# A Mamba block with two gated layers: what follows the scan, from its first norm on, one tick later, and a broadcast copy moved from VectorE to ScalarE

## The chip, the cores and the metric

The kernel runs on one core of a Trainium2 chip. A core has five engines that each work through their own instruction stream in order: TensorE (PE in the profile; its weight loads are PEld), VectorE (DVE), ScalarE (ACT), GpSimd (POOL) and SyncE (SP), which here issues nearly all DMAs. [...] The metric is device time in microseconds (us) of one execution. Before the change three runs gave 1165.02, 1166.05 and 1168.84 us; the median is 1166.05 us.

## What is computed

The input is 4 sequences of 1024 tokens with 256 features, all float32. Cut to what matters:

```python
x = x + mamba_block(layernorm(x))
x = x + ffn(layernorm(x))

# mamba_block(v):
#   u = rmsnorm(v);  z, xs, B, C, dt_raw = split(u @ in_proj)
#   dt = softplus(dt_raw @ dt_proj + b)
#   for each token t:   h = exp(dt_t * A) * h + (dt_t * xs_t) * B_t     (8192 states per sequence)
#                       y_t = sum over states of h * C_t
#   h1 = v + ((y + xs * D) * silu(z)) @ out_proj
#   return h1 + (silu(rms(h1) @ gate) * (rms(h1) @ up)) @ down          (704 hidden)
# ffn(v):  (hadamard(silu(v @ W1) * (v @ W3))) @ W2                     (1024 hidden)
```

The Hadamard transform is folded into W2 at the start (the tile `w2h`), so that it costs nothing later.

## The kernel before

**Units and ticks.** The 4 x 1024 tokens are cut into 8 units of 512 tokens, two per sequence (`us`); units 1, 3, 5 and 7 carry the state on from units 0, 2, 4 and 6. Each unit's scan is cut into 16 steps q of 128 partitions x 4 states x 512 tokens, 128 steps in all. The program is written out by a loop over ticks (L857 to L893), two ticks to a step: tick t belongs to step q = t // 2 and to its first or second half. Unit k is scanned in ticks 32k to 32k+31. This text calls the tick's number within its unit its **place**, 0 to 31.

**What each tick does.** VectorE multiplies the input by B (`times_b`, L765, tile `bx` in PSUM) and runs two scans (`scan`, L774) over two of the step's four states. ScalarE takes the exponentials of the next step, two per tick (`exp`, L741, in place in the tile `da`). GpSimd multiplies the previous step's states by C once per step (`times_c`, L784). TensorE sums them over the states once per step (`sum_states`, L795, eight rows in the trace, tile `py`); that of step q is entered in the second tick of step q+1. SyncE fetches the next tiles: `da` (1 MB, broadcast from memory; four buffers, so the DMA for step q+4 waits for the sum of step q), `ub`, `cr`.

**What else is woven in.** `at(tick, lane, f)` puts a piece of work into a tick, and the lanes say where in the tick it stands: "PE" and "ACT" first, "ACTb" after `times_b`, then the tick's two exponentials; "DVE" stands between the tick's two scans; "POOL" after `times_c`; "PEend" after `sum_states`; "ACTend", "SP" and "SPend" last. Since every engine runs in order, the tick and the lane decide what waits behind what. Two helpers add the dense work:

- `pre(u, H)` prepares the unit that is scanned from tick H on: the norm of x (`un`, L363), its transposes (`transposes`, L213), and projections (`pe_x` and others, through `project`, L226), their copies (`act_x`), and the DMAs that spread them (`dma_xb`, `dma_xr`).
- `post(u, E, other)` finishes a unit whose scan ended at tick E, so it runs beside the next unit's scan: the residual rows (`hr`), the output projection (`wo`, L306 through `add_rows`), the norm's sums (`row_stats`, L173), `small2` on GpSimd, the first normed rows (`hn` with "r3"), their transposes and copies (`ht`), the first gated layer (`gated`, weights `wg`, `wu`, tile `m`), its down projection (`wd`), `small3`, `hn` with "r4", its transposes and copies (`xt`), the second gated layer (`w1`, `w3`, tile `g`), its down projection (`w2h`), and the store.

`gated` takes three chunks at a time: three gate projections, then the `z` projection of a later unit where there is one (`zs`), then three up projections, two to a tick. ScalarE applies SiLU to the three gate projections (`silus`, L263), and copies the up projections out (`up`, L270); GpSimd multiplies (`product`, L274). All projections and transposes go through a ring of four PSUM buffers (`dense`), so a projection waits for the copy of the one four before it.

**The last link of a half unit.** After eight steps `py` is complete. `sum_states` then enters `y_dx` (L810) on VectorE, four ticks after the last step began: at place 18 for the first half of the unit being scanned, at place 2 for the second half of the unit before. `y_z` (L815) follows on GpSimd, and at place 2 and 3 the output projection.

**B's broadcast.** For every half unit the tile `pb` (one PSUM bank, one buffer) gets a copy of the fetched rows `br` (`copy_b`, L754). It may be written only after the last `times_b` of the old half (place 15 or 31), and the first `times_b` of the new one (place 16 or 0) reads it. Before the change VectorE makes the copy at place 15 (between its two scans), ScalarE that at place 31 (lane "ACTb").

Of the kernel before, what the change touches and what calls it, by code (L numbers as in the profile page):

```python
# [11 lines left out]
ALU = mybir.AluOpType  # L12
# [15 lines left out]
def tile_block(ctx: ExitStack, tc: tile.TileContext, a, out):  # L28
# [20 lines left out]
    nc = tc.nc  # L49
# [15 lines left out]
    def dense_psum():  # L65
        return ps_m.tile([P, T], F32, tag="dense", name="dense")
# [14 lines left out]
    us = [{"b": b, "c": c} for b in range(BATCH) for c in range(SEQ // T)]  # L81
# [80 lines left out]
    def row_stats(u, src, ts, centred=True):  # L162

        if 0 in ts:
            u["mv"] = sm.tile([P, 2, TT], F32, tag="mv", name="mv")
        for t in ts:
            junk = p1.tile([P, DM], F32, tag="junk", name="junk")
            nm, ms = u["mv"][:, 0, t : t + 1], u["mv"][:, 1, t : t + 1]
            if centred:
                nc.scalar.activation(  # L170
                    junk, src[:, t, :], AF.Identity, scale=-1.0 / (16 * DM), accum_out=nm
                )
            nc.scalar.activation(  # L173
                junk,
                src[:, t, :],
                AF.Square,
                bias=nm if centred else 0.0,
                scale=1.0 / 16,
                accum_out=ms,
            )  # L180
# [13 lines left out]
    def rsqrt_eps(dst, var):  # L194
        nc.gpsimd.tensor_scalar(dst, var, EPS, 1.0, ALU.add, ALU.mult)
        nc.gpsimd.tensor_tensor(dst, dst, mhalf, ALU.pow)

    def scaled_rows(dst, src, scale, bias, ts):
        for t in ts:
            nc.scalar.activation(  # L200
                dst[:, t, :],
                src[:, t, :],
                AF.Identity,
                bias=bias[:, t : t + 1] if bias is not None else 0.0,
                scale=scale[:, t : t + 1],
            )

    def transposes(u, src):

        u["pt"] = [dense_psum() for _ in range(2)]  # L210
        for k in range(2):
            for t in range(TT):
                nc.tensor.transpose(  # L213
                    u["pt"][k][:, t * P : (t + 1) * P], src[:, t, k * P : (k + 1) * P], ident
                )
# [22 lines left out]
    def at(tick, lane, fn, *args):  # L238
        todo[tick][lane].append(partial(fn, *args))
# [98 lines left out]
    def pre(u, H):  # L338

        s = {}  # L340
# [217 lines left out]
        if H == 32:  # L558

            at(0, "ACTend", lambda: row_stats(u, u["x"], (0, 1)))  # L560
            at(1, "ACTend", lambda: row_stats(u, u["x"], (2, 3)))
            at(3, "POOL", small)
            at(5, "POOL", small_end)
            at(4, "ACT", un, (0, 1))
            at(5, "ACT", un, (2, 3))
            at(6, "PE", lambda: transposes(u, s["un"]))
            at(6, "ACTend", transposed, u, "ut")
        else:
            at(H - 54, "SP", load_x, u)
            at(H - 45, "ACTend", lambda: row_stats(u, u["x"], (0, 1)))  # L570
            at(H - 43, "ACTend", lambda: row_stats(u, u["x"], (2, 3)))
            at(H - 39, "POOL", small)
            at(H - 37, "POOL", small_end)
            at(H - 32, "ACT", un, (0, 1))
            at(H - 31, "ACT", un, (2, 3))
            at(H - 30, "PE", lambda: transposes(u, s["un"]))
            at(H - 30, "ACTend", transposed, u, "ut")
        at(H - 24, "PE", pe_x)
        at(H - 23, "ACT", act_x)
        at(H - 22, "SP", dma_xb)  # L580
        at(H - 19, "SPend", dma_xr, 0)
        at(H - 17, "SPend", dma_xr, 1)
        at(H - 16, "PE", pe_dt)
        at(H - 16, "PE", pe_c, 0)
        if H == 32:
            for h in range(2):
                at(H - 11, "PE", pe_z, h)
# [16 lines left out]
    def post(u, E, other):  # L604


        s = {}

        def hr(ts):
            if 0 in ts:  # L610
                u["hr"] = p2.tile([P, TT, DM], F32, tag="hr", name="hr")
            scaled_rows(u["hr"], u["x"], u["r1"], u["nm1"], ts)

        def small2():
            t = sm.tile([P, 2, TT], F32, tag="s2", name="s2")
            r3 = t[:, 1, :]
            rsqrt_eps(r3, u["mv"][:, 1, :])
            s["r3"] = r3

        def small3():  # L620
            t = sm.tile([P, 2, TT], F32, tag="s2", name="s2")
            nm, r4 = t[:, 0, :], t[:, 1, :]
            nm16, var = u["mv"][:, 0, :], u["mv"][:, 1, :]
            rsqrt_eps(r4, var)
            nc.gpsimd.tensor_tensor(nm, nm16, r4, ALU.mult)
            nc.gpsimd.tensor_scalar(nm, nm, 16.0, None, ALU.mult)
            s["r4"], s["nm"] = r4, nm

        def hn(scale, bias):
            s["tok"] = p1.tile([P, TT, DM], F32, tag="tok", name="hn")  # L630
            scaled_rows(s["tok"], u["hr"], s[scale], s[bias] if bias else None, range(TT))

        def big(name):
            u[name] = p1.tile([P, 8, T], F32, tag="big", name=name)

        def store():
            b, c = u["b"], u["c"]
            nc.sync.dma_start(
                out=out[b, c * T : (c + 1) * T, :].rearrange("(t p) d -> p t d", p=P), in_=u["hr"]
            )  # L640

        at(E + 3, "ACT", hr, (0, 1))
        at(E + 4, "ACT", hr, (2, 3))
        add_rows(
            E + 3,
            u,
            lambda: [u["yt"][:, k, :] for k in range(2)],
            lambda: [W["wo"][:, k, :] for k in range(2)],
            4,
            "PEend",  # L650
            on_pool=u is not us[-1],
        )
        at(E + 5, "ACTend", lambda: row_stats(u, u["hr"], (0, 1), False))
        at(E + 6, "ACTend", lambda: row_stats(u, u["hr"], (2, 3), False))
        at(E + 7, "POOL", small2)
        at(E + 8, "ACT", hn, "r3", None)
        at(E + 9, "PE", lambda: transposes(u, s["tok"]))
        at(E + 9, "ACTend", transposed, u, "ht")
        at(E + 9, "POOL", lambda: nc.gpsimd.tensor_tensor(u["hr"], u["hr"], u["x"], ALU.add))
        at(E + 10, "PE", big, "m")  # L660
        sizes = [min(P, DFF - c * P) for c in range(6)]
        chunks = list(enumerate(sizes))
        for i in range(2):
            gated(E + 10 + 3 * i, u, "m", "wg", "wu", chunks[3 * i : 3 * i + 3], "ht",
                  (other, i) if other else None)
        add_rows(
            E + 18,
            u,
            lambda: [u["m"][:n, c, :] for c, n in enumerate(sizes)],
            lambda: [W["wd"][:n, c, :] for c, n in enumerate(sizes)],  # L670
            1,
        )
        at(E + 20, "ACTend", lambda: row_stats(u, u["hr"], (0, 1)))
        at(E + 22, "ACTend", lambda: row_stats(u, u["hr"], (2, 3)))
        at(E + 23, "POOL", small3)
        at(E + 24, "ACT", hn, "r4", "nm")
        at(E + 25, "PE", lambda: transposes(u, s["tok"]))
        at(E + 25, "ACTend", transposed, u, "xt")
        at(E + 26, "PE", big, "g")
        chunks8 = [(c, P) for c in range(8)]  # L680
        for i in range(3):
            gated(E + 26 + 3 * i, u, "g", "w1", "w3", chunks8[3 * i : 3 * i + 3], "xt")
        add_rows(
            E + 36,
            u,
            lambda: [u["g"][:, c, :] for c in range(8)],
            lambda: [w2h[:, c, :] for c in range(8)],
            1,
            on_pool=u is not us[-1],
        )  # L690
        at(E + 43, "SPend", store)


    an = nega.rearrange("p (h j b a) -> p h j b a", h=2, j=4, b=4)
    NQ = 16 * len(us)
# [52 lines left out]
    def carry_of(s):  # L748
        return s["u"]["carry"][:, s["h"], s["j"], :, s["g"]]

    def copy_b(q):
        u, h = qs[q]["u"], qs[q]["h"]
        u["pb"] = ps_b.tile([P, T], F32, tag="b", name="pb")
        (nc.vector.tensor_copy if h else nc.scalar.copy)(u["pb"], u["br", h])  # L754

    def times_b(q, b0):
        s = qs[q]
# [60 lines left out]
    for k, u in enumerate(us):  # L818
        pre(u, 32 * k)
    for k, u in enumerate(us):  # L820
        post(u, 32 * k + 32, us[k + 2] if k + 2 < len(us) else None)
# [26 lines left out]
        at(10 + i, "PE", hadamard_end, 2 * i)  # L848
    for q in range(8, NQ, 8):
        at(2 * q - 8, "SPend", dma_br, q)  # L850

        at(2 * q - 1, "DVE" if q // 8 % 2 else "ACTb", copy_b, q)

    def has(q):
        return 0 <= q < NQ
# [2 lines left out]
    while todo:  # L858
        q, half = divmod(tick, 2)
# [102 lines left out]
```

## Time and profile before

| | |
|---|---|
| median of three runs | 1166.05 us (1165.02 to 1168.84) |
| the profiled execution | 1173.07 us, span 1171.2 us |
| mean granted TensorE clock | 0.899 |
| first scan of unit 1 to unit 7 begins at | 158.67, 285.07, 415.20, 543.38, 671.46, 800.02, 925.55 us |
| last scan ends | 1053.7 us; the rest is unit 7's `post` alone |
| `times_b` | 1.23 us each, two per step |
| `scan` | 1.21 us (units 0, 2, 4, 6) or 1.27 us (units 1, 3, 5, 7), four per step |
| `times_c` | 4.53 us per step |
| `exp` | 0.71 us, four per step |
| `copy_b` | 0.67 us on VectorE (8), 0.60 us on ScalarE (7) |
| `sum_states` | about 1.0 us per step on a TensorE at full clock |
| one matmul of 128x512 | 0.45 us a row, two rows for each matmul of the code (float32) |
| ScalarE's load of a function table | 1.28 us, 90 in all |

A step lasts 7.4 us in units 0, 2, 4, 6 and 7.65 us in the others where nothing is waited for. In the profile's tables every row has the engine, the line, the operation, out<-in by the program's names, and shapes. In a timeline the first column is the start, the second the duration of a merged group, and the bracket at the end gives how long the engine sat idle before it and what ended that.

### The profile page before, as it was taken

To read this page: it belongs to the slowest core of one execution; us is meant where nothing else is said; L and a number is where in the kernel's file an instruction comes from. 1 tells how busy PE (TensorE), PEld (TensorE's weight loads), DVE (VectorE), ACT (ScalarE), POOL (GpSimd) and SP (SyncE) were. 2 spreads that over 40 slices of the span, in tenths; PEclk is the share of its full clock that TensorE was granted. 3 is DMA by queue.
4 is the path that set the end of the run, shared out by engine and by line. 5 is a ranking of instruction groups with operands and counts; after the bars stand their busy time and mean duration, and the time that the engine had idled before them with its cause. 6 is when DMAs were issued, how large, how long until landed. Compare 5 with 4: busy or idle time off the path is not lost.

```text
span 1171.2 us, 11883 instructions
## 1 busy us (share of the span) xinstructions
PE 959.6 (82%) x3374; PEld 456.5 (39%) x3374; DVE 962.9 (82%) x840; ACT 782.2 (67%) x1411; POOL 887.1 (76%) x515
## 2 busy tenths in 40 slices
PE   8464236969998799969996999979997987799978
PEld 3121012423634255423633364424543362336535
DVE  4897799999998989999999899999999899990000
ACT  3835556868768786779677786878685967563331
POOL 6675758878978888878977998789977898674312
PEclk9777558979899799979998899979997999789989
DMA  7989999898799889997799889988799789730000
GB/s 252 352 300 351 353 327 308 311 325 296 250 340 320 300 298 320 319 327 281 270 348 325 281 300 334 319 325 297 270 310 360 281 291 343 262 111 1 18 0 18
DMA packets 89441, 321.89 MB, mean 275 GB/s; under 512 B 9312, under 2 KB 20000, under 8 KB 73120
## 3 DMA queue, kind: packets, MB, share of 16 engines
q1 hardware_dynamic: 87520, 318.38, 77.1%
q10 hardware_dynamic: 1856, 2.75, 0.7%
q8 instruction: 27, 0.44, 0.1%
q14 instruction: 38, 0.31, 0.1%
HBM read 302.22 MB, written 18.87 MB: 274 GB/s over the span
## 4 chain that ended last, share of the span: by engine, by line
PE 25%; DMA 7%; DVE 6%; POOL 6%; issue 5%; ACT 4%; DVEq 0%; POOLq 0%; ACTq 0%; SPq 0%
PE dense L226 14%; PE dense L306 8%; DMA da<-dtd 5%; POOL da L784 4%; DVE da L774 3%; DVE bx L765 3%; PE py L795 3%; DMA ub<-ud 2%; ACT da L741 1%; POOL m L274 1%; POOL g L274 1%; DVE hr L316 0%; ACT up L270 0%; ACT L741 0%; ACT junk L173 0%
## 5 line engine op out<-in xcount | busy, mean ns | idle before, releaser
L784 POOL TENSOR_TENSOR da<-da,cr 128x2048 f32<-128x2048 f32 x128 | 580.0, 4531 | 86.8 <-DVE da L774 22.5
L741 ACT ACTIVATE da<-da,nega 128x512 f32<-128x512 f32 x508 | 334.4, 713 | 170.8 <-DMA da<-dtd 159.3
L774 DVE TENSOR_TENSOR_SCAN da<-da,carry,bx 128x512 f32<-128x512 f32 x256 | 315.7, 1268 | 20.0 <-DVE bx L765 7.6
L774 DVE TENSOR_TENSOR_SCAN da<-da,bx 128x512 f32<-128x512 f32 x256 | 300.2, 1209 | 37.0 <-ACT da L741 21.3
L765 DVE TENSOR_TENSOR bx<-ub,pb 128x1024 f32<-128x1024 f32 x254 | 312.2, 1229 | 20.3 <-ACT pb L754 9.3
L795 PE MATMUL py<-da,rsel 128*32 128x512 f32 x1024 | 162.5, 712 | 159.4 <-POOL da L784 159.4
L226 PE MATMUL dense<-xt,w 128*128 128x512 f32 x512 | 238.4, 621 | 1.4 <-ACT si L263 1.4
L226 PEld LDWEIGHTS dense<-xt,w 128*128 128x128 f32 x512 | 99.4, 199 | 145.9 <-issue 123.4
L795 PEld LDWEIGHTS py<-da,rsel 128*32 128x32 f32 x1024 | 21.4, 115 | 243.0 <-POOL da L784 201.2
L306 PE MATMUL dense<-w2h,g 128*128 128x256 f32 x512 | 113.4, 380 | 0.0
L274 POOL TENSOR_TENSOR g<-si,up 128x512 f32<-128x512 f32 x64 | 80.5, 1272 | 32.3 <-ACT up L270 32.2
L306 PEld LDWEIGHTS dense<-w2h,g 128*128 128x128 f32 x512 | 96.8, 190 | 18.4 <-ACT ev L321 2.5
L306 PE MATMUL dense<-wd,m 128*128 128x256 f32 (+1 forms) x384 | 98.2, 400 | 0.9 <-POOL m L274 0.9
L316 DVE TENSOR_TENSOR hr<-hr,dense 128x512 f32<-128x512 f32 x20 | 13.4, 669 | 99.9 <-PE dense L306 99.9
L226 PE MATMUL dense<-ut,win 128*128 128x512 f32 x192 | 94.7, 625 | 0.2 <-ACT ut L220 0.2
L270 ACT COPY up<-dense 128x512 f32<-128x512 f32 x112 | 63.4, 579 | 46.8 <-PE dense L226 46.4
L274 POOL TENSOR_TENSOR m<-si,up 128x512 f32<-128x512 f32 (+1 forms) x48 | 60.2, 1270 | 43.5 <-ACT up L270 43.5
L226 PE MATMUL dense<-ht,wg 128*128 128x512 f32 x192 | 87.7, 600 | 3.4 <-ACT ht L220 3.4
L306 PEld LDWEIGHTS dense<-wd,m 128*128 128x128 f32 (+1 forms) x384 | 68.6, 192 | 37.6 <-issue 20.6
L263 ACT ACTIVATE si<-dense 128x512 f32<-128x512 f32 x112 | 60.7, 596 | 28.4 <-PE dense L226 25.5
L226 PE MATMUL dense<-ht,wu 128*128 128x512 f32 x160 | 72.8, 600 | 4.8 <-ACT si L263 4.8
L741 ACT ACT_TABLE_LOAD x44 | 56.5, 1283 | 4.8 <-DMA da<-dtd 4.0
(95 smaller groups left out, 798.6 us busy)
## 6 DMA issues: line engine op xcount, KB each, us to landing
da<-dtd SPq DMA_DIRECT2D x127, 1024.0 KB
ub<-ud SPq DMA_DIRECT2D x254, 512.0 KB
cr<-cd SPq DMA_DIRECT2D x64, 256.0 KB
x<-in_x SPq DMA_DIRECT2D x8, 512.0 KB
dtd<-dt SPq DMA_DIRECT2D x16, 256.0 KB
ud<-du SPq DMA_DIRECT2D x16, 256.0 KB
cd<-cc SPq DMA_DIRECT2D x16, 256.0 KB
out<-hr SPq DMA_DIRECT2D x8, 512.0 KB
```

The costliest lines, as they stand in the source:

```text
L226: nc.tensor.matmul(dst[:n], lhsT=w[:, k, col : col + n], rhs=src[:, k, :], start=(k == 0), stop=(k == 1),)
L263: nc.scalar.activation(g[i]["si"][:n], g[i]["pg"][:n], AF.Silu)
L270: nc.scalar.copy(g[i]["up"][:n], g[i]["pu"][:n])
L274: nc.gpsimd.tensor_tensor(u[dst][:n, c, :], g[i]["si"][:n], g[i]["up"][:n], ALU.mult)
L306: nc.tensor.matmul(po[t // 2][:, t % 2, :], lhsT=left[k][:, t * P : (t + 1) * P], rhs=right[k], start=(k == 0), stop=(k == n - 1),)
L316: nc.vector.tensor_tensor(hr, hr, po[i], ALU.add)
L741: nc.scalar.activation(da, da if q else s["u"]["pdt", b], AF.Exp, scale=an[:, s["h"], s["j"], b, s["g"] : s["g"] + 1],)
L765: nc.vector.tensor_tensor(s["bx"], s["ub", b0 // 2], u["pb"].unsqueeze(1).broadcast_to([P, 2, T]), ALU.mult)
L774: nc.vector.tensor_tensor_scan(da, da, s["bx"][:, b % 2, :], start, ALU.mult, ALU.add)
L784: nc.gpsimd.tensor_tensor(s["da"], s["da"], s["cr"].unsqueeze(1).broadcast_to([P, 4, T]), ALU.mult)
L795: nc.tensor.matmul(u["py"][32 * b : 32 * b + 32, :], lhsT=rsel[:, 2 * s["j"] + s["g"], :], rhs=s["da"][:, b, :], start=first, stop=last,)
```

## The change

For the six units 0 to 5, everything of `post` from the first `hn` on is entered one tick later (`F = E + 1`); what comes before it (`hr`, the output projection, `row_stats`, `small2`) stays, and units 6 and 7 keep all their ticks. The second `hn` goes to lane "ACTend" in those six. In `pre`, for units 2 to 7, `un` and its transposes are entered two ticks later; for units 1 to 7 `pe_x`, `act_x`, `dma_xb`, `dma_xr`, `pe_dt` and the first `pe_c` one tick later. `copy_b` at place 15 is made by ScalarE (lane "ACTb") for units 1 to 6; VectorE keeps it for units 0 and 7. `y_dx`, `y_z` and all of the scan itself keep their ticks.

```diff
@@ pre
-            at(H - 32, "ACT", un, (0, 1))
-            at(H - 31, "ACT", un, (2, 3))
-            at(H - 30, "PE", lambda: transposes(u, s["un"]))
-            at(H - 30, "ACTend", transposed, u, "ut")
-        at(H - 24, "PE", pe_x)
-        at(H - 23, "ACT", act_x)
-        at(H - 22, "SP", dma_xb)
-        at(H - 19, "SPend", dma_xr, 0)
-        at(H - 17, "SPend", dma_xr, 1)
-        at(H - 16, "PE", pe_dt)
-        at(H - 16, "PE", pe_c, 0)
+            at(H - 30, "ACT", un, (0, 1))
+            at(H - 29, "ACT", un, (2, 3))
+            at(H - 28, "PE", lambda: transposes(u, s["un"]))
+            at(H - 28, "ACTend", transposed, u, "ut")
+        at(H - 23, "PE", pe_x)
+        at(H - 22, "ACT", act_x)
+        at(H - 21, "SP", dma_xb)
+        at(H - 18, "SPend", dma_xr, 0)
+        at(H - 16, "SPend", dma_xr, 1)
+        at(H - 15, "PE", pe_dt)
+        at(H - 15, "PE", pe_c, 0)
@@ post: all from here on with F in place of E
-        at(E + 8, "ACT", hn, "r3", None)
+        F = E + (us.index(u) < len(us) - 2)
+        at(F + 8, "ACT", hn, "r3", None)
...
-        at(E + 24, "ACT", hn, "r4", "nm")
+        at(F + 24, "ACTend" if F > E else "ACT", hn, "r4", "nm")
...
-        at(E + 43, "SPend", store)
+        at(F + 43, "SPend", store)
@@
+    def by_vector(q):
+        return q in (8, NQ - 8)
...
-        (nc.vector.tensor_copy if h else nc.scalar.copy)(u["pb"], u["br", h])
+        (nc.vector.tensor_copy if by_vector(q) else nc.scalar.copy)(u["pb"], u["br", h])
...
-        at(2 * q - 1, "DVE" if q // 8 % 2 else "ACTb", copy_b, q)
+        at(2 * q - 1, "DVE" if by_vector(q) else "ACTb", copy_b, q)
```

More of the change, by code (lines that the diff above doesn't have):

```diff
@@ L655, in post @@
         at(E + 7, "POOL", small2)
-        at(E + 8, "ACT", hn, "r3", None)
[L657 to L660, printed above, removed]
+        F = E + (us.index(u) < len(us) - 2)
+        at(F + 8, "ACT", hn, "r3", None)
+        at(F + 9, "PE", lambda: transposes(u, s["tok"]))
+        at(F + 9, "ACTend", transposed, u, "ht")
+        at(F + 9, "POOL", lambda: nc.gpsimd.tensor_tensor(u["hr"], u["hr"], u["x"], ALU.add))
+        at(F + 10, "PE", big, "m")
         sizes = [min(P, DFF - c * P) for c in range(6)]
@@ L663, in post @@
         for i in range(2):
-            gated(E + 10 + 3 * i, u, "m", "wg", "wu", chunks[3 * i : 3 * i + 3], "ht",
+            gated(F + 10 + 3 * i, u, "m", "wg", "wu", chunks[3 * i : 3 * i + 3], "ht",
                   (other, i) if other else None)
         add_rows(
-            E + 18,
+            F + 18,
             u,
@@ L672, in post @@
         )
-        at(E + 20, "ACTend", lambda: row_stats(u, u["hr"], (0, 1)))
-        at(E + 22, "ACTend", lambda: row_stats(u, u["hr"], (2, 3)))
-        at(E + 23, "POOL", small3)
-        at(E + 24, "ACT", hn, "r4", "nm")
-        at(E + 25, "PE", lambda: transposes(u, s["tok"]))
-        at(E + 25, "ACTend", transposed, u, "xt")
-        at(E + 26, "PE", big, "g")
+        at(F + 20, "ACTend", lambda: row_stats(u, u["hr"], (0, 1)))
+        at(F + 22, "ACTend", lambda: row_stats(u, u["hr"], (2, 3)))
+        at(F + 23, "POOL", small3)
+        at(F + 24, "ACTend" if F > E else "ACT", hn, "r4", "nm")
+        at(F + 25, "PE", lambda: transposes(u, s["tok"]))
+        at(F + 25, "ACTend", transposed, u, "xt")
+        at(F + 26, "PE", big, "g")
         chunks8 = [(c, P) for c in range(8)]
         for i in range(3):
-            gated(E + 26 + 3 * i, u, "g", "w1", "w3", chunks8[3 * i : 3 * i + 3], "xt")
+            gated(F + 26 + 3 * i, u, "g", "w1", "w3", chunks8[3 * i : 3 * i + 3], "xt")
         add_rows(
-            E + 36,
+            F + 36,
             u,
```

## The prediction

> **What bounds the kernel now.** I read the page first, then VectorE's waits, then the timelines around the longest of them. The page's first lines:
>
> ```profile
> span 1171.2 us, 11883 instructions
> PE 959.6 (82%) x3374; PEld 456.5 (39%) x3374; DVE 962.9 (82%) x840; ACT 782.2 (67%) x1411; POOL 887.1 (76%) x515
> ```
>
> VectorE and TensorE are equally busy over the span. By stretch it looks different: from unit 1's first scan to the last scan (158.7 to 1053.7 us) VectorE runs almost without a hole, so there every hole is time. The holes, from the view of waits kept to VectorE (total us, times, longest):
>
> ```profile
> DVE da L774 <- ACT da L741: 21.5, 18, 4.2
> DVE yt L810 <- PE py L795: 12.5, 7, 8.9
> ...
> DVE bx L765 <- ACT pb L754: 9.3, 3, 4.1
> ```
>
> The third line is the change's target: at place 0 of units 3, 5 and 7 VectorE waits 3.16, 4.09 and 2.04 us for ScalarE's copy. Of the first line, unit 0 has 15.2 us, and 5.1 us lie at places 14 to 17 of units 2, 4 and 6 (0.70 and 3.05; 0.91; 0.39). The second line looks small (8.9 of it is the tail), but decides. VectorE's timeline where unit 5 begins:
>
> ```profile
> 671.46 1.23 DVE L765 TENSOR_TENSOR bx<-ub,pb 128x1024 f32<-128x1024 f32 x1 [4.09 <-ACT pb L754]
> ...
> 682.90 0.75 DVE L810 SCALAR_TENSOR_TENSOR yt<-xr,dpar,py 128x512 f32<-128x512 f32 x1 [0.95 <-PE py L795]
> ```
>
> After it lost 4.09 us, VectorE still had to wait at `y_dx` for TensorE. In the trace the last row of a half's sum ends 0.15 us before `y_dx` starts six times: at places 18 of units 2, 4, 6 and at places 2 of units 3, 5, 7. So at these six points TensorE's chain sets the time, and a hole filled ahead of them only becomes a longer wait there. At the other `y_dx` the sum is early by 3.68, 3.42, 2.97 us (place 18 of units 1, 3, 5) and 1.12, 0.75, 1.09 us (place 2 of units 2, 4, 6). TensorE's timeline shows why: ahead of `y_dx` it runs in one piece.
>
> ```profile
> 648.99 8.59 PE L226 MATMUL dense<-xt,w 128*128 128x512 f32 x16
> 657.50 1.07 PE L795 MATMUL py<-da,rsel 128*32 128x512 f32 x8
> 658.50 7.13 PE L226 MATMUL dense<-xt,w 128*128 128x512 f32 x16
> 665.57 1.07 PE L795 MATMUL py<-da,rsel 128*32 128x512 f32 x8
> 666.56 7.13 PE L226 MATMUL dense<-xt,w 128*128 128x512 f32 x16
> 673.62 1.07 PE L795 MATMUL py<-da,rsel 128*32 128x512 f32 x8
> 674.62 7.13 PE L226 MATMUL dense<-xt,w 128*128 128x512 f32 x16
> 681.68 1.07 PE L795 MATMUL py<-da,rsel 128*32 128x512 f32 x8
> ```
>
> A step takes 7.4 to 7.65 us, one such group 8.1 us: TensorE falls behind through the second gated layer, and `y_dx` waits for the last sum.
>
> **The change, part by part.** I work in differences to before, at the `y_dx` points.
>
> *Copies.* Six copies leave VectorE: 6 x 0.67 = 4.0 us of work. They stand at place 15, so `y_dx` at place 18 comes next. In unit 1 the sum is 3.68 us early: **-0.7**. Elsewhere they are counted in the next paragraphs. ScalarE gets 6 x 0.60 us. The copy moves behind the last `times_b` of the half, so ScalarE's two exponentials of the tick queue behind it; they are needed two ticks on, which covers it. At place 31 the copy now has neither `silus` nor `up` ahead of it in its tick; the 9.3 us go if the exponentials ahead arrive.
>
> *What stands in front.* The parity matters. The first pair of exponentials of a step waits for its `da` (160 us in the waits of ScalarE); the second pair doesn't. Before, `hn`, `ht`, `xt` and the first `silus` stood ahead of a step's first pair; one tick later they stand behind a first pair. ScalarE's rows around place 26 of unit 3 to 4 and of unit 4 to 5 have the same form:
>
> ```profile
> 646.67 1.04 ACT L220 COPY xt<-dense 128x512 f32<-128x512 f32 x2
> 652.06 2.56 ACT L741 ACTIVATE da<-da,nega 128x512 f32<-128x512 f32 x4 [4.34 <-DMA da<-dtd]
> ```
>
> The copies of `xt` ran, then ScalarE idled 4.34 us for `da`. In the new order they come after that wait. Likewise `small3`'s tick moves past one `times_c` (4.53 us) on GpSimd.
>
> *Place 23 to place 2, into units 2, 4, 6.* Into unit 4: place 23's scans end at 512.05. `times_c` to 516.7, `small3` (1.95) to 518.7, `hn` (2.07) to 520.8, the transposes follow it to about 521.5, but ahead of the copy stand the exponentials that began at 523.02 for want of `da`: one pair to 524.3, the first `xt` copy to 524.9. Four matmuls stand before the next sum (eight before): 8 x 0.45 = 3.6, plus 1.8 from a slow start (8.90 us for the same group at 518.64 against 7.13 warm), to 530.3; then 1.0 and three times 8.07, so the last sum ends at 555.5 where it ended at 552.72. It is 2.8 late against slacks of 1.12, 0.75 and 1.09: 1.7 + 2.0 + 1.7 = **+5.4**. Bounds: 0 if `da` comes 2.8 earlier; +3.3 each if 1.6 later.
>
> *Place 23 to place 2, into units 3, 5, 7.* Before, this took 44.52, 45.45 and 43.40 us, because `times_c` stood behind `small3`, which waited for `row_stats`: at unit 4, GpSimd idled 5.24 us and `times_c` began at 642.54 instead of about 637.5. That goes. The same chain as above from 637.44 gives 47.2 us if `da` lands as before (652.06): 653.4 the pair, 654.0 the copy, 659.4 the matmuls, 684.6 `y_dx`. It gives 41.1 if `da` no longer matters. The middle, 44.2, is about the 44.5 that it was on average: **0**, bounds -3.4 and +2.7 each.
>
> *Place 3 to place 18, units 3 and 5.* The last four up matmuls (3.6) now stand behind the half's last sum, ahead of `wo`, and `un`'s transposes (1.09) between `wo` and `w2h`. In unit 3 the sum ended at 426.49, so: up to 430.1, one sum 431.1, `wo` 3.5, `un` 1.1, `w2h` from 435.7 instead of 433.39: +2.3. `w2h`'s last chunk now waits for one `times_c` more, but only its seventh and eighth matmul need it, and that is just in time (438.3). Then `ht`: equal. Then the first up projection finds all four PSUM buffers taken until a SiLU. That stood ready before; now it follows exponentials whose `da` comes 7.8 to 9.8 us after a sum (457.38 and 473.53 in unit 3): 456.4 + 8.8 + 1.33 + 1.28 + 0.5 = 468.3, while TensorE is there at 466.3: +2.0 (0 to 3.4). Together +4.3, against a slack of 3.42 and 2.97 less the 0.67 of the copy: stalls of 1.55 and 2.0, and with the copy's 0.67 taken off +0.9 and +1.3, **+2.2** (bounds -1.3 and +5).
>
> *Place 3 to place 18, units 2, 4, 6.* No slack here. The same moves cost only +0.2, since `wo` and `w2h`'s first half took 12.0 us there, 1.7 over their 24 matmuls at 0.43. The SiLU wait is again 0 to 3.4, I take 1.8: +2.0 in units 4 and 6. Unit 2 already had such a wait (1.78 us at 350.57): 0. **+4.0** (bounds -1.6 and +8.5). The 5.1 us of waits for exponentials go or are swallowed by this.
>
> *DMAs.* `xbd`, `xr` and the store keep their sizes and pass at most one `ub` on SP's queue. `xr` is read five ticks (18 us) after its issue, more than any wait for `da` above; nothing is late. The tail of units 6 and 7 keeps its ticks: 0.
>
> **Sum.** -0.7 + 5.4 + 0 + 2.2 + 4.0 = +10.9 us. Against the profiled execution: 1173.07 + 10.9 = 1184.0; that one lies 7.0 above the median, so at the median 1166.05 + 10.9 = **1177.0 us**.
>
> [...]
>
> **Rivals.**
> 1. *Faster.* TensorE's chain is not lengthened, because `da` lands before the moved ScalarE work needs it. It decides at `xt`: if `da` is there by the end of the transposes (2.8 us earlier), hardly a term above is positive. For it: four buffers, and the stalls themselves give DMA time. Against it: `da`'s DMA waits for TensorE's own sums. All low bounds: -0.7 + 0 - 10.2 - 1.3 - 1.6 = -13.8, so 1152. Chance 0.33.
> 2. *The holes trade places.* Waits at `pb` turn into equal waits at `y_dx`: 1166. Chance 0.12. A measurement can tell about 0.3% (3.5 us) from no change.
> 3. *The ring.* Later sums make `da` late, and scans wait for exponentials as well; the high bounds, -0.7 + 9.9 + 8.1 + 5 + 8.5 = +30.8, can't all hold, since a wait at one `y_dx` gives time to the chain of the next; two thirds of it, +20.5, gives 1187. Chance 0.12.
> 4. *The change does nothing.* VectorE's stream of the changed kernel holds two copies of `pb` instead of eight, so it does move; ScalarE's holds 90 table loads as before, so nothing is added there. Chance 0.
>
> **How the numbers follow.** My forecast has 0.43, rival 3 0.12: slower 0.55; same 0.12; faster 0.33. To leave out no more than 0.2, the range reaches from rival 1's time to rival 3's: 1152 to 1187. The forecast's own range is 1170 to 1184.
>
> **What would show it.** Right: no wait for `pb` over 1 us; longer waits of `yt` L810 for `py`, at place 18 of units 3 to 6 and place 2 of units 2, 4, 6; TensorE idle before `ht,wu` for `si`; `xt` behind exponentials. Wrong: `yt` waits no longer than before, the 4.0 us of copies show in the steps' length, and units 2, 4, 6 shrink below 126 us.

## The result, and the profile after

The changed kernel takes 1182.99 us (median of four runs, 1178.42 to 1184.42) against 1165.53 us for the kernel before (four runs): a ratio of 1.0138, 95% interval 1.0101 to 1.0175, so it is slower by some 17 us. The profiled execution after took 1183.34 us with a span of 1181.6 us, at a granted clock of 0.897, where before it was 0.899. The page's line of busy times:

```profile
PE 959.4 (81%) x3374; PEld 455.4 (39%) x3374; DVE 959.9 (81%) x834; ACT 786.6 (67%) x1417; POOL 887.3 (75%) x515
```

The work is the same on every engine to 5 us; VectorE has six instructions fewer, ScalarE six more. All of the difference is waiting. VectorE's waits:

```profile
DVE yt L816 <- PE py L801: 34.0, 13, 9.9
DVE da L780 <- ACT da L743: 17.5, 21, 4.8
...
DVE bx L771 <- ACT pb L760: 3.2, 3, 1.5
```

The wait for the copy of B fell from 9.3 to 3.2 us, as it was meant to. The wait of `y_dx` for TensorE's sum rose from 12.5 to 34.0 us; without the tail (8.9 and 9.9) that is 3.6 to 24.1. Six of these waits, 2.84 to 2.95 us each, stand at place 18 of units 1 to 6; the rest, 0.27 to 2.10 us, at place 2 of units 2 to 7. Unit 4's place 18 in VectorE's timeline:

```profile
622.29 0.75 DVE L816 SCALAR_TENSOR_TENSOR yt<-xr,dpar,py 128x512 f32<-128x512 f32 x1 [2.95 <-PE py L801]
```

TensorE's timeline of the same moment, first before, then after: what stands between the half's last two sums, and as the last line the sum that releases `y_dx`:

```profile
610.51 1.98 PE L406 MATMUL dense<-raw,dtw 128*128 128x512 f32 x4
612.34 1.88 PE L226 MATMUL dense<-ut,win 128*128 128x512 f32 x4
614.69 1.06 PE L795 MATMUL py<-da,rsel 128*32 128x512 f32 x8 [0.48 <-POOL da L784]
```

```profile
613.33 3.70 PE L226 MATMUL dense<-ht,wu 128*128 128x512 f32 x8
616.87 1.88 PE L406 MATMUL dense<-raw,dtw 128*128 128x512 f32 x4
619.16 1.98 PE L226 MATMUL dense<-ut,win 128*128 128x512 f32 x4 [0.41 <-ACT up L270]
621.08 1.06 PE L801 MATMUL py<-da,rsel 128*32 128x512 f32 x8
```

Before, 8 rows stood there, and the last sum even waited 0.48 us for GpSimd. After, up projections (`ht,wu`, 8 rows) stand there too, since they moved a tick past the earlier sum, and TensorE is the last to arrive. This is the obvious reading; the first theory below is made of it.

**A ledger.** I cut each unit's cycle in two at TensorE. The **run** goes from the first transpose for `xt` (`hn` with "r4") to the end of the last sum before place 18's `y_dx`; the **way** goes from there to the next `xt` transpose. In it VectorE walks its ticks up to place 23, and `times_c`, `small3` and `hn` follow. Worked out from the traces, means over the five cycles that begin with the `xt` of units 1 to 5's scans; the idle time is the sum of TensorE's pauses of more than 0.15 us:

| profiled execution | its time | run | TensorE idle in it | way | both |
|---|---|---|---|---|---|
| before | 1173.07 | 102.6 | 4.7 | 25.7 | 128.3 |
| after | 1183.34 | 100.3 | 4.4 | 29.5 | 129.9 |

"Both" is by definition the length of a unit, so the ledger explains nothing by itself; it shows where a unit grew. The way is 3.8 us longer, one tick; the run gave 2.3 us back.

Why the way is longer can be read at the end of it. Before, where unit 4's scan runs (all engines, lines of TensorE, GpSimd and ScalarE chosen):

```profile
640.31 0.19 POOL L195 TENSOR_SCALAR s<-mv 128x4 f32<-128x4 f32 x1 [5.24 <-ACT junk L173]
...
642.24 1.09 ACT L200 ACTIVATE hn<-hr,s 128x256 f32<-128x256 f32 x2 [0.31 <-POOL s L626]
...
642.90 0.47 PE L213 MATMUL dense<-ident,hn 128*128 128x128 f32 x1 [5.84 <-ACT hn L200]
```

After:

```profile
644.00 0.19 POOL L789 COPY carry<-da 128x4 f32<-128x4 f32 x1 [3.16 <-DVE da L780]
644.27 4.52 POOL L790 TENSOR_TENSOR da<-da,cr 128x2048 f32<-128x2048 f32 x1
...
648.87 0.19 POOL L195 TENSOR_SCALAR s<-mv 128x4 f32<-128x4 f32 x1
...
650.80 1.09 ACT L200 ACTIVATE hn<-hr,s 128x256 f32<-128x256 f32 x2 [3.14 <-POOL s L626]
...
651.46 0.48 PE L213 MATMUL dense<-ident,hn 128*128 128x128 f32 x1 [0.68 <-ACT hn L200]
```

Before, `small3` (L195) stands ahead of a `times_c` and waits for `row_stats` (5.24 us); the transposes begin at 642.90, which is 27.1 us after the sum (the longest of the five ways before, which go from 23.7 to 27.1). After, `small3` stands behind a `times_c` that starts when VectorE has finished place 23 (643.93; the small copy of `carry` ahead of it waited 3.16 us for that), and ScalarE waits 3.14 us for `small3`; the transposes begin 29.3 us after the sum (622.14). So `xt` now hangs on VectorE's ticks, and VectorE hangs on TensorE's last sum at place 18.

### The profile page after: what moved, and what is told of

Its sections match the earlier page's. It is cut to its first block, busy times and chain, and to the rows that moved or that the text cites. A ratio compares the mean times of both kernels' runs of the same rounds, so it can differ in the third digit from the quotient of the medians.

```text
span 1181.6 us, 11882 instructions
## 1 busy us (share of the span) xinstructions
PE 959.4 (81%) x3374; PEld 455.4 (39%) x3374; DVE 959.9 (81%) x834; ACT 786.6 (67%) x1417; POOL 887.3 (75%) x515
## 4 chain that ended last, share of the span: by engine, by line
PE 42%; ACT 15%; DMA 15%; POOL 9%; DVE 9%; issue 8%; SPq 1%; DVEq 0%; POOLq 0%; ACTq 0%
PE dense L226 27%; PE dense L306 10%; DMA da<-dtd 8%; POOL da L790 7%; ACT da L743 6%; PE py L801 5%; DVE da L780 5%; DVE bx L771 4%; DMA cr<-cd 3%; ACT up L270 1%; ACT L743 1%; ACT L263 1%; DMA ub<-ud 1%; DMA w<-in_w 1%; ACT si L263 1%
## 5 line engine op out<-in xcount | busy, mean ns | idle before, releaser
L801 PE MATMUL py<-da,rsel 128*32 128x512 f32 x1024 | 155.8, 684 | 168.8 <-POOL da L790 168.7
L226 PE MATMUL dense<-xt,w 128*128 128x512 f32 x512 | 245.0, 633 | 3.0 <-ACT xt L220 3.0
L306 PE MATMUL dense<-w2h,g 128*128 128x256 f32 x512 | 115.8, 383 | 6.8 <-ACT ut L220 6.2
L316 DVE TENSOR_TENSOR hr<-hr,dense 128x512 f32<-128x512 f32 x20 | 13.4, 670 | 100.3 <-PE dense L306 100.3
L226 PE MATMUL dense<-ht,wu 128*128 128x512 f32 x160 | 76.4, 617 | 11.1 <-ACT si L263 11.1
L226 PEld LDWEIGHTS dense<-ut,win 128*128 128x128 f32 x192 | 37.7, 205 | 59.6 <-issue 42.6
```

Of the source, the lines that this page charges most:

```text
L226: nc.tensor.matmul(dst[:n], lhsT=w[:, k, col : col + n], rhs=src[:, k, :], start=(k == 0), stop=(k == 1),)
L306: nc.tensor.matmul(po[t // 2][:, t % 2, :], lhsT=left[k][:, t * P : (t + 1) * P], rhs=right[k], start=(k == 0), stop=(k == n - 1),)
L316: nc.vector.tensor_tensor(hr, hr, po[i], ALU.add)
L801: nc.tensor.matmul(u["py"][32 * b : 32 * b + 32, :], lhsT=rsel[:, 2 * s["j"] + s["g"], :], rhs=s["da"][:, b, :], start=first, stop=last,)
```

## The theories

- **P**, the obvious one: the matmuls between the last two sums hold `y_dx` at place 18; take them away, or `y_dx` later, and the time comes back.
- **C**: ScalarE's copies hold its exponentials and `pb`. **L**: late `da` sets the rhythm.
- **D**, a loop: the length of way plus run, of which the second gated layer's tick lengthened the way. It was formed after the first four runs, of which two had spoken against P, with two rivals: **U**, the moves in `pre`, and **A**, the alignment, that is, which work of ScalarE stands behind a pair of exponentials that waits for `da`.

Every kernel is compared with the kernel before on the same chip, whose medians there were 1166.36 us (first four experiments), 1164.24 us (next four) and 1164.91 us (last four).

## The experiments

**The change without its copies.**

```diff
-        return q in (8, NQ - 8)
+        return q // 8 % 2 == 1
```

> The change without its copies: all of the shift by a tick, but VectorE copies pb at place 15 as before. Theory P (TensorE's row ahead of the last sum of place 18 is longer by the shift, and y_dx waits 2.8 to 2.95 us there in units 1 to 6): the copy's 0.67 us falls into that wait, so the time stays within 2 us of the changed kernel, 1181 to 1185 us, with y_dx idle some 2.2 us instead of 2.9 at place 18. Rival C (ScalarE's copy delays the exponentials and pb): the time falls back to about 1166 us.

Measured: 1181.66 us, ratio 1.0126 (1.0106 to 1.0146). The time is as P has it; C falls. The waits of `yt` are 30.7 us instead of 34.0, but not as P has it: at place 18 of units 1, 3 and 5 they are 1.41, 2.86 and 1.90 us, and at that of units 2, 4 and 6 still 2.95. In the changed kernel the copies are worth nothing that can be measured.

**The copies alone.** In the kernel before:

```diff
-        (nc.vector.tensor_copy if h else nc.scalar.copy)(u["pb"], u["br", h])
+        (nc.vector.tensor_copy if q in (8, NQ - 8) else nc.scalar.copy)(u["pb"], u["br", h])
...
-        at(2 * q - 1, "DVE" if q // 8 % 2 else "ACTb", copy_b, q)
+        at(2 * q - 1, "DVE" if q in (8, NQ - 8) else "ACTb", copy_b, q)
```

> The kernel before with only the copies moved to ScalarE in units 1 to 6. Theory P: where the sum was early (place 18 of units 1, 3, 5) 0.67 us is saved each, elsewhere it turns into a longer wait of y_dx: -2 us in all, 1162 to 1166 us. Rival C: the time rises by a good part of the change's 17 us, to 1175 or more. Full worth of the copies: -4.0 us.

Measured: 1171.70 us, ratio 1.0042 (1.0019 to 1.0066). Neither: they cost some 5 us where 2 to 4 were to be gained. Except for the tail and 0.28 us, no `y_dx` waits, and the idle time stands elsewhere:

```profile
DVE bx L765 <- ACT pb L754: 19.6, 6, 4.9
```

All six waits (1.25 to 4.86 us) are at place 16: ScalarE reaches its copy of place 15 late, behind a SiLU, a `zs` and an `up` of the first gated layer, and the last two wait for TensorE (0.45 and 1.18 us in unit 4). The copy was taken off an engine that was waiting and put on one whose queue was longer.

**Projections behind the last sum.** In the changed kernel:

```diff
-        at(H - 15, "PE", pe_dt)
-        at(H - 15, "PE", pe_c, 0)
+        at(H - 14, "PE", pe_dt)
+        at(H - 14, "PE", pe_c, 0)
...
-        at(H - 15, "ACT", act_dt, 0)
-        at(H - 15, "ACT", act_dt, 1)
-        at(H - 14, "ACT", act_c, 0)
-        at(H - 13, "POOL", make_u, 0, nc.gpsimd)
-        at(H - 13, "SPend", dma_dt, 0)
+        at(H - 14, "ACT", act_dt, 0)
+        at(H - 14, "ACT", act_dt, 1)
+        at(H - 13, "ACT", act_c, 0)
+        at(H - 12, "POOL", make_u, 0, nc.gpsimd)
+        at(H - 12, "SPend", dma_dt, 0)
```

> The changed kernel with pe_dt, the first pe_c and what follows them (act_dt, act_c, make_u, dma_dt) one tick later again, so that these four matmuls (3.9 us with their wait) stand behind the last sum of place 18 and no longer ahead of it. Theory P: the six waits of y_dx at place 18 (17.4 us) go, as the sum is 3.9 us earlier and the wait was 2.9; what is left at place 2 is 6.6 us as before: 1183 - 17 = 1166 us, down to 1162 if the copies count as well, up to 1172 if the wait moves to place 2. Rival L (late da sets the rhythm, y_dx only shows it): no more than 4 us of gain, since the scans then wait for da at places 18 and 19.

Measured: 1188.46 us, ratio 1.0184 (1.0156 to 1.0213). The six waits of `y_dx` at place 18 went to 0.00 us, as P says, and the time did not come back: the ratio lies above the change's 1.0138, though the two intervals overlap. (The scan just ahead of `y_dx` waits 1.2 to 1.4 us in units 1, 2, 4, 5 and 6; in the changed kernel it waits 1.42 us in units 2, 4 and 6.) The waits came back at place 2, where `y_dx` now waits 3.51 to 4.24 us in each of units 2 to 7. The trace points to the start of TensorE's run, where TensorE waits for `xt` 20.9 us in five units and waited 2.7 us in the changed kernel (TensorE, then ScalarE):

```profile
658.54 6.12 PE L226 MATMUL dense<-xt,w 128*128 128x512 f32 x7 [4.91 <-ACT xt L220]
```

```profile
656.69 1.33 ACT L743 ACTIVATE da<-da,nega 128x512 f32<-128x512 f32 x2 [4.44 <-DMA da<-dtd]
657.93 1.05 ACT L220 COPY xt<-dense 128x512 f32<-128x512 f32 x2
```

The copies of `xt` stand behind a pair of exponentials whose `da` has not landed (2.29 to 4.92 us in units 1 to 6), the mechanism that the prediction described. P, as the cause of the loss, falls; L's number holds, and here its `da` is seen, though at `xt` and not at the scans of places 18 and 19.

**`y_dx` of place 18 a tick later.** In the changed kernel:

```diff
-            at(2 * q + 4, "DVE", y_dx, u, s["h"])
-            at(2 * q + 5, "POOL0", y_z, u, s["h"])
+            at(2 * q + 4 + (s["h"] == 0), "DVE", y_dx, u, s["h"])
+            at(2 * q + 5 + (s["h"] == 0), "POOL0", y_z, u, s["h"])
```

> The changed kernel with y_dx and y_z of the first half (place 18) entered one tick later; nothing else is moved. Theory P: the tick gives TensorE 3.7 us, more than the wait of 2.9, so the waits at place 18 go and the time is 1166 to 1170 us; the next sum (place 19) needs py freed and starts up to 1.2 us later, which costs nothing on VectorE. Rival L: TensorE and VectorE both hang on late da, the idle time reappears at scans behind it, 1178 us or more.

Measured: 1180.64 us, ratio 1.0124 (1.0101 to 1.0147). Again the waits of `y_dx` at place 18 are gone (0.00 us, the sum over 3.3 us early), and the time has not come back. VectorE waits 34.2 us for exponentials instead of 17.5: in units 2 to 6 at places 18 (0.85 to 1.42 us) and 19 (2.53 to 2.65). Unit 4, VectorE and then ScalarE:

```profile
619.86 1.22 DVE L780 TENSOR_TENSOR_SCAN da<-da,bx 128x512 f32<-128x512 f32 x1 [2.65 <-ACT da L743]
```

```profile
610.91 0.59 ACT L270 COPY up<-dense 128x512 f32<-128x512 f32 x1 [2.37 <-PE dense L226]
...
616.53 1.27 ACT L415 ACTIVATE dt<-dense,dtb 128x512 f32<-128x512 f32 x2
617.81 1.28 ACT L743 ACT_TABLE_LOAD   x1
619.11 1.33 ACT L743 ACTIVATE da<-da,nega 128x512 f32<-128x512 f32 x2
```

L's number (1178 or more) fits, its mechanism doesn't: no `da` is late here. ScalarE's rows stand one behind the other: its `up` waits 2.37 us for TensorE, `act_dt` follows with two table loads (3.83 us), and the exponentials that VectorE needs queue behind. In the changed kernel the same wait lies hidden under that of `y_dx`, 2.95 us. So TensorE's lateness has a second path to VectorE, and takes it once `y_dx` is out of the way.

**The second part back, with a faster `wd`.** In the changed kernel `wd`'s row blocks are entered two to a tick, so that all from the second `row_stats` on can stand in the ticks of before (G = E):

```diff
-            1,
+            2 if us.index(u) < len(us) - 2 else 1,
...
-        at(F + 20, "ACTend", lambda: row_stats(u, u["hr"], (0, 1)))
+        G = E
+        at(G + 20, "ACTend", lambda: row_stats(u, u["hr"], (0, 1)))
...
-        at(F + 24, "ACTend" if F > E else "ACT", hn, "r4", "nm")
+        at(G + 24, "ACT", hn, "r4", "nm")
```

> The changed kernel, but with wd's four row blocks in two ticks instead of four, so that everything from the second row_stats on (small3, hn, xt, the second gated layer, w2h) can stand in the ticks of the kernel before; the first gated layer and pre stay a tick late and the copies stay on ScalarE. Theory D (a loop through xt): from the first xt transpose on TensorE has one almost unbroken run to the last sum at place 18 (100.5 us a unit after the change), and from that sum VectorE's ticks up to place 23, times_c, small3 and hn lead to the next xt (29.5 us, before the change 25.9); a unit lasts as long as the two together. So 29.5 falls back by about 3.6 us in each of five to six units: 1183 - 18 to 22 = 1161 to 1166 us. Theory P (the matmuls ahead of the last sum of place 18): these are unchanged, so at least 1178 us.

Measured: 1190.51 us, ratio 1.0226 (1.0201 to 1.0251). D's size for the way was even exceeded (22.3 us), but the run grew to 110.0 us, with 9.8 us of TensorE's idle time in it. P's number (1178 or more) holds, and the waits at place 18 are still there (2.89 to 2.95 us in units 2 to 6), but P has nothing for a time above that of the changed kernel. D as I had put it, with a run of fixed length, falls. What fills the run (TensorE, then ScalarE):

```profile
593.21 5.73 PE L226 MATMUL dense<-ht,wg 128*128 128x512 f32 x8 [4.63 <-ACT ht L220]
```

```profile
591.36 1.33 ACT L744 ACTIVATE da<-da,nega 128x512 f32<-128x512 f32 x2 [4.17 <-DMA da<-dtd]
```

TensorE is early, but `ht` is still a tick late, behind exponentials that wait for `da`. The first gated layer's tick has its own tie to VectorE's ticks, and it takes over when `xt`'s is loosened.

**The second part alone, a tick late.** In the kernel before, G = E + 1 for units 0 to 5 from the second `row_stats` on, `hn` in lane "ACTend":

```diff
-        at(E + 20, "ACTend", lambda: row_stats(u, u["hr"], (0, 1)))
+        G = E + (us.index(u) < len(us) - 2)
+        at(G + 20, "ACTend", lambda: row_stats(u, u["hr"], (0, 1)))
...
-        at(E + 24, "ACT", hn, "r4", "nm")
+        at(G + 24, "ACTend" if G > E else "ACT", hn, "r4", "nm")
```

> The kernel before with only the part from the second row_stats on (small3, hn, xt, second gated layer, w2h, store) a tick later in units 0 to 5; no copies, first gated layer and pre as before. Theory D: the way from the last sum of place 18 to the next xt grows by up to a tick (3.7 us) in each unit, against which TensorE's run loses the 2 to 4 us in which it waited for times_c: 1170 to 1182 us. Theory P: the matmuls ahead of the sum at place 18 are those of the kernel before, so 1166 us or less.

Measured: 1182.28 us, ratio 1.0143 (1.0118 to 1.0169). This part alone gives a loss as large as that of the change, without copies, without the first layer's up projections between the last sums, and with `y_dx` waiting no more than 0.25 us at place 18. The way is 30.1 us. The waits are at place 2 instead, 4.24 us in units 3, 5 and 7. (Its profiled execution, 1175.36 us, is the fastest of its six, and that of before lies 7 us above its median: run and way of the two add up to the same 128.3 us, so these two traces do not hold most of the 18 us.)

The same size is not yet the same loss. Cut by stretches of VectorE, from place 2 of unit 1 to place 2 of unit 7, the two kernels lose in different places (worked out from the traces, us):

| profiled execution | places 2 to 18 | places 18 to 23 | places 23 to 2 | together |
|---|---|---|---|---|
| before | 379.6 | 131.1 | 257.3 | 768.1 |
| after | 395.7 | 131.9 | 251.1 | 778.7 |
| the second part alone | 377.3 | 131.1 | 264.0 | 772.4 |

The second part alone loses behind place 23, where ScalarE waits for `da` ahead of the copies of `xt` (3.45, 4.39, 1.63 and 3.60 us in units 2, 4, 5 and 6; at most 0.72 us in the changed kernel). The whole change gains there and loses between places 2 and 18, where `w2h` and the first gated layer stand.

**`pre`'s moves alone.** The kernel before with the lines of the change in `pre`, nothing else.

> The kernel before with pre's moves alone (un and its transposes two ticks later, pe_x, act_x, the DMAs, pe_dt and pe_c one tick later). Theory D: nothing on the way from sum to xt moves, and TensorE's run holds the same matmuls: 1163 to 1169 us. Rival U (un's transposes between wo and w2h cost 1.2 us of wait a unit and late projections do the rest): 1173 us or more.

Measured: 1169.09 us, ratio 1.0047 (1.0027 to 1.0068). At the edge of D's band and below U's: they cost some 5 us, not nothing and not the loss. Way and run are 25.0 and 103.2 us, which is a unit as long as in the profile of before (128.2 against 128.3); since that one lies 7 us above its median, these profiles don't tell where the 5 us stand.

**A tick earlier than before.** As the version with the faster `wd` in the changed kernel, with G = E - 1 (the first `row_stats` stays at E + 20):

> As the first kernel of this call, with the part from the second row_stats (tokens 2, 3) on one tick earlier still, thus a tick before the kernel before. Theory D: the way from the sum to xt falls by another tick to 22 us until VectorE's own 118 to 120 us of work a unit and its small gaps (4 us) are the bound: 1145 to 1162 us, below both kernels. Theory P: as the first kernel, 1178 us or more.

Measured: 1212.41 us, ratio 1.0414 (1.0390 to 1.0438). The way is 22.3 us again, not shorter, and the run 113.8 us with 11.8 us of idle time: TensorE waits before `ht,wg` (5.7 to 6.8 us) and before `w2h` for `g` (2.8 to 3.1 us). D's forecast was wrong by 50 us, for the same reason as above.

**The second part two ticks late.** In the kernel before, G = E + 2, `hn` in its own lane "ACT":

> The kernel before with the part from the second row_stats on two ticks later instead of one (hn in its own lane again, so that xt stands ahead of a step's first pair of exponentials as in the kernel before). One tick later gave 1182 us. Theory D (the way from the last sum of place 18 to the next xt): the way is two ticks longer than before, up to 33 us, so 1190 to 1205 us. Theory A (the alignment: one tick puts the copies of xt behind exponentials that wait for da, two ticks put them ahead of them again): back to 1164 to 1172 us.

Measured: 1188.53 us, ratio 1.0207 (1.0190 to 1.0225). A falls: with `xt` ahead of the exponentials again the time doesn't come back. The way is 32.7 us as D says, the run 98.9; the time is a little below D's band, since the second tick costs only 6 us more.

**The first part back.** In the changed kernel the lines from `hn` with "r3" to the first `gated` have E in place of F; all from `wd` on stays late.

> The changed kernel with the first gated layer (hn with r3, ht, wg, wu, m) back in the ticks of the kernel before; wd and all behind it stay a tick late, as do pre and the copies. Theory D: the way from sum to xt stays as long as after the change (29.5 us): 1178 to 1184 us. Theory P (matmuls ahead of the last sum of place 18): the up projections stand ahead of the sum before it again, the waits of 2.9 us go: 1166 to 1170 us.

Measured: 1190.89 us, ratio 1.0208 (1.0181 to 1.0235). No `y_dx` waits at place 18, the up projections stand where they stood, P's forecast is missed by 21 us and D's by 7: the way is 32.9 us, not 29.5. The waits are now at place 2 (2.69 to 4.20 us in units 3 to 7) and at place 16 (4.16 to 5.70 us in units 2 to 6), there once more through ScalarE's queue (VectorE, then ScalarE):

```profile
613.10 1.23 DVE L771 TENSOR_TENSOR bx<-ub,pb 128x1024 f32<-128x1024 f32 x1 [5.69 <-ACT pb L760]
```

```profile
611.99 0.59 ACT L270 COPY up<-dense 128x512 f32<-128x512 f32 x1 [1.18 <-PE dense L226]
612.48 0.60 ACT L760 COPY pb<-br 128x512 f32<-128x512 f32 x1
```

**A faster `wd` in the kernel before.** Only `wd`'s `per_tick` is changed, by the first two lines of the diff above.

> The kernel before with wd's four row blocks in two ticks instead of four (units 0 to 5); no tick of anything else is moved. Theory D: row_stats no longer holds small3, and times_c behind it, so that the way from sum to xt falls from 25.9 to about 22.3 us as it did with wd so in the changed kernel; ht is not late here, so the run does not grow by that: VectorE's own 119 us and 4 us of small gaps a unit are the bound, 127 to 124.5 us: 1150 to 1162 us. Rival: the run grows by what the way loses, since VectorE's ticks hold ht: 1164 us, within 4.

Measured: 1167.85 us, ratio 1.0032 (1.0019 to 1.0045). The rival's time is right, but neither mechanism is seen: the way did not fall (25.8 us, 25.7 before), and the run did not grow (102.0). The 44.5 us from place 23 to place 2 into units 3, 5 and 7 became 41.1 to 41.4; against it VectorE's own additions of `wd` now wait for TensorE at places 19 and 20 of units 2, 4 and 6 (1.39 and 1.57 us), so that places 18 to 23 take 24.7 us there instead of 21.5:

```profile
DVE hr L316 <- PE dense L306: 109.5, 12, 44.6
```

This was 99.9 us in 6 waits before. The hole changed its place.

**The same, the second part a tick earlier.** G = E - 1 in the kernel before, with the faster `wd`:

> As the third kernel of this call, with the second row_stats of tokens 2, 3 and all behind it one tick earlier. Theory D: the way falls no further than VectorE allows, 1150 to 1162 us. Rival: with xt a tick earlier its copies stand behind exponentials that wait for da and w2h comes before its products are there, as in the kernel with the changed first layer (1212 us): 1180 us or more.

Measured: 1203.32 us, ratio 1.0336 (1.0309 to 1.0363), a time as the rival said. Of its reasons one is seen: TensorE idles before `w2h` for `g` (3.7 to 4.0 us a unit), and also before `ht,wu` for `si`. The other is not, for the exponentials just ahead of the copies of `xt` waited no more than 0.13 us; the way is 25.0 and the run 109.1 us.

No version tried is faster than the kernel before.

**What follows.** Shown: the second part's tick alone is enough for a loss as large as the change's (1.0143 and 1.0138); the copies add nothing to the change's (1.0126 without them); and the six waits at place 18 are where the loss stands, not why, since three kernels without them have ratios of 1.0124, 1.0184 and 1.0208. Not shown: that the second part's tick is the cause in the changed kernel. The two lose in different stretches, the first layer's tick was never run alone, and the version with the second part back lost more (1.0226), while the faster `wd` that it needs cost little in the kernel before (1.0032): with that `wd`, the first layer's tick, `pre`'s moves and the copies are enough for a loss as well. Read from the traces: `xt` hangs on VectorE's place 23, the second layer then fills TensorE into the next unit, and its lateness is passed on to VectorE by `y_dx`, by the exponentials behind `up` and `act_dt`, or by `pb` behind `up`, whichever stands first. Open: why the parts' costs (4.9 for `pre`, 5.3 for the copies, 18 for the second part, by the medians) add up to 28 us and the change costs 17. That they share waits is likely, but no run tried just two of the three together. Whether an earlier `da`, which L needs, would loosen the chain was not tried either. D's numbers held in none of the eight runs that tested it; three missed narrowly (the second part alone by 0.28 us, `pre` alone by 0.09, two ticks late by 1.47). Its one-sidedness is what the runs show: a later second part made every kernel slower, as D says, but an earlier one (way 22.3 and 25.0 us) made none faster, since the run filled with other waits.

## Why the prediction was right, and where it was not

The direction and the range held, and so did the reason at large as to where the time would stand: `y_dx` released by TensorE went from 6 points to 12, and the filled holes became longer waits there. From place 2 of unit 1 to place 2 of unit 7 the changed kernel's profiled execution needs 778.7 us where the one before needed 768.1: +10.6 against a forecast of +10.9. But the terms behind that sum did not hold; errors of both signs met, and that they cancelled is luck.

- *Copies, unit 1 (-0.7).* Wrong: place 3 to place 18 of unit 1 grew by 2.37 us and `y_dx` waits 2.84. The step said that the sum is 3.68 us early and stopped there; the first layer's move, which I counted in units 2 to 6, makes it late in unit 1 too.
- *Place 23 to place 2, units 2, 4, 6 (+5.4).* +0.93, +0.02, +0.18: 1.1. The chain was right in its order (`times_c`, `small3`, `hn`, then `xt` behind exponentials) and in the end of `hn`, 8.8 us after place 23's scans in the sum and in the trace. But I let the exponentials wait for `da` until 10.97 us after them, and in these three units they began with the end of `hn`: `da` had landed, and the low bound that I had named was near. Only into unit 5 did they wait at all (ScalarE after):

```profile
650.80 2.08 ACT L200 ACTIVATE hn<-hr,s 128x256 f32<-128x256 f32 x4 [3.14 <-POOL s L626]
653.59 1.33 ACT L743 ACTIVATE da<-da,nega 128x512 f32<-128x512 f32 x2 [0.72 <-DMA da<-dtd]
```

- *Place 23 to place 2, units 3, 5, 7 (0).* -2.66, -2.99, -1.72: -7.4. Between -3.4 and +2.7 I took the middle; `da` was nearly in time (ScalarE waited 0.72 us for it at `xt` of unit 4 to 5, where it had been 4.34), so the low end was the right one.
- *Place 3 to place 18 (+2.2 and +4.0).* +3.03 and +2.07 in units 3 and 5, and +1.02, +3.05, +4.50 in units 2, 4, 6: 13.7 against 6.2. **This step failed.** It followed `w2h`, `ht` and the first up projection, and ended there. It did not count that the up projections of the last chunks, 8 rows or 3.70 us, come to stand between the last two sums, beside `pe_dt` and `pe_c`. The wait for `si` that it did name is there, 8.2 us where it was 3.7; a wait of 6.2 us before `w2h`, for `ut`'s copies, where it was none, it had not named:

```profile
PE py L801 <- POOL da L790: 50.2, 18, 7.2
PE dense L226 <- ACT si L263: 8.2, 5, 2.2
PE dense L306 <- ACT ut L220: 6.2, 5, 1.2
PE dense L213 <- ACT hn L200: 3.4, 5, 0.7
```

(Waits of TensorE after, from place 2 of unit 2 to place 2 of unit 7.) The last line is a gain: it was 18.4 us before. The first line took most of it back: the sums' waits for `times_c` were 37.4 us before.

- *The account itself.* The text added up what each stretch loses. By the experiments that is not how this kernel pays: take one stretch's loss away, and another has it. By terms, the errors were +3.1 (copies), -4.3, -7.4 and +7.5 us, and places 18 to 23, which had no term, grew by 0.7.
- *At the median.* I took 7.0 us off both times, since the execution profiled before lay that far above its median. The one after lies 0.35 us above its own. So the medians differ by 17 us where the profiles differ by 10.3, and the forecast, 1177.0, is 6 us low, so that the sum meets the one profile of before and not the kernel's usual time. The changed kernel's units are regular (129.6 to 130.0 us for units 2 to 6, from `y_dx` at place 2 to the next), those of before were not (126.8 to 131.5): it fits that a chance wait is swallowed there by one that comes anyway, but no run shows it.
- *What would show it.* Longer waits of `yt` at the named places, TensorE idle for `si`, and `xt` behind exponentials are all seen, the last without the wait for `da` that was to make it dear. Against the forecast, two waits for `pb` are over 1 us (1.17 and 1.50, at place 16 of units 2 and 6).
- *VectorE relieved.* The six copies, 4.0 us of VectorE's work, moved off it alone, cost 5 us. For `y_dx` at place 18 the sum was made earlier once, and `y_dx` itself entered later once: the gap of 2.9 us became one of 3.5 to 4.2 at place 2, or one of 2.6 at place 19.

## What to carry to other kernels

A wait's name says where the idle time stands. Whether it is the cause is known only when it has been taken away and the time has come back; here three kernels lost the wait and kept the time. When engines wait for each other in a cycle, follow one whole cycle and ask what a move does to its length, before pricing the stretches. Here that gave the right sign for a later tick, and neither the sign for an earlier one nor a right time. A tick added at a point that every unit passes can cost up to a tick in every unit. And before moving work off the busiest engine, read what the receiving engine's queue waits for at that place: ScalarE's copy of 0.60 us stood behind work that waited for TensorE, and VectorE waited up to 5.70 us for it.

## What was not expected of the hardware

Around a pause of 6.89 us TensorE's granted clock went from 1.00 to 0.50, and later back to 1.00. In the table by stretches after (length, then the engines' busy times, then the clock, the DMA share and GB/s), around the `xt` transposes at 651.46:

```profile
651.00:657.00 6.00, 4.31 (x10) 2.31 (x11) 5.74 (x6) 5.28 (x10) 5.61 (x6) 0.50 0.91 344
657.00:663.00 6.00, 6.00 (x18) 2.07 (x17) 5.73 (x6) 3.76 (x6) 5.52 (x7) 0.80 0.44 167
663.00:680.00 17.00, 17.00 (x52) 6.63 (x51) 16.06 (x14) 13.56 (x21) 14.91 (x9) 1.00 0.76 270
```

From 642.3 on, in the pause of 6.89 us before 648.84, the clock is 0.50, then 0.80, then 1.00. The 0.80 is a mean: taken apart, the stretch has 0.50 up to 659.3 and 1.00 from 659.4 on, 3.9 us after TensorE began to work without a pause (655.45). After the change each of units 1 to 6 has one such time at 0.50 near its `xt`, some 14 to 17 us long; before the change each has one there too, as long, and in unit 4 the first 16 rows for `xt`, from 648.99 on, took 8.59 us and the next 16 rows 7.13.

ScalarE's change of table cost 1.30 us from its load to the start of what needed it (616.53 after 615.23, in the kernel with `y_dx` later), and two such loads of 1.28 us stand around `act_dt` there, at 615.23 and 617.81: that is why it can hold the exponentials up.

And one kernel on one chip varied by more than I had allowed for: 17 executions of the kernel before took 1159.84 to 1168.42 us.
